# Gate, up and down of an adaLN block: where the last pair's operands, Wd's slices, Silu's products and down's first loads stand

## The chip, the cores and the metric

The kernel runs on one core of one Trainium2 chip, in one launch. The metric is the device time of that launch in microseconds, as the median of runs; all arithmetic is fp32.

## The reference

The kernel computes one transformer block with adaptive layer norm, for x of 2 × 1024 × 1024. Cut to what matters:

```python
mod = (silu(c) @ wmod).reshape(2, 6, 1, -1)
sa, ca, ga, sb, cb, gb = (mod[:, i] for i in range(6))
h = layernorm(x) * (1 + ca) + sa
x = x + ga * attention(h)               # 32 heads, causal, ALiBi slopes, clipped qkv, LN on q and k
h = layernorm(x) * (1 + cb) + sb
gate = einsum('bsh,ih->bsi', h, Wg) * ag        # Wg, Wu: 2752 x 1024
up = einsum('bsh,ih->bsi', h, Wu) * au
x = x + gb * (einsum('bsi,hi->bsh', silu(gate) * up, Wd) * ad)   # Wd: 1024 x 2752
```

(`ga` and `gb` are kept at least 0.25 away from zero.) The change touches the second half: gate, up and down.

## The kernel before

The large products are done by Strassen and Winograd's scheme with seven products in place of eight, in two levels: an outer one whose seven products are called stages (`STAGES`), and an inner one whose seven products run in the order of `CHAIN`. The reduction over 1024 becomes, for gate and up, stage by stage, products of a weight tile (an inner operand, made by `gate_inner` on GpSimd from the outer sums of `gate_sums`) with a 512 KB tile of h's operand.

**h's operands.** The tokens of h lie transposed in SBUF, in two batch halves (b = 0, 1) and pairs j = 0 to 3. For the outer operands T1 to T4 and B22 of a pair, `second_batch` (L1299) makes four half sums, and for each operand `inner_b` (L1156) makes four inner differences into a tile `inner` (two buffers) and stores all to DRAM (`bop_B..`, `bop_T..`). Pairs 0 to 2 share this between VectorE and GpSimd; the last one, `second(3, nc.vector)`, is called after the first weights' loads and does everything on VectorE. It runs in the pool `rest`, which also serves the rest rows (the 192 rows of the inner dimension of 2752 that the slabs do not cover), and which is closed before gate and up get their pools.

**Gate and up.** There are five slabs s of 512 of the inner dimension. Each has seven stages, and each stage seven inner products. One inner product is, for gate and for up, two matmuls of 128x128 by 128x512; both use one `bt` tile (`moving`, L1635, six buffers), loaded by SyncE except the first six, which ScalarE's queue loads. Banks are `gx, gy, ux, uy`, in two sets of four that alternate by stage. `merge` (L1560) reads a bank after its product: P1, U2 and P5 become parts (copied on ScalarE or added on VectorE, L1566 and L1568), the others become results X, C, Z and T (L1572, L1574, L1576). A bank's next product waits for the read.

**After a stage.** `after(n, go)` puts a closure into a queue that `run_due` empties n products later in program order. `final` (L1678) applies Silu on ScalarE (L1683) and the product on VectorE (L1684) to a finished result and stores it for down (`act_dram`, L1688). GpSimd makes T and Z from X (L1730, L1737). At the end of a slab eight act sums S1 to S4 (L1751) are made on VectorE and stored (L1752).

**Wd's slices.** Down needs outer sums of Wd. In twenty slices, one for each stage from the first, `down_load` (L1170) loads 512 KB into the single tile `wdr` with two DMAs, and `down_weights` (L1179), five products later, makes T1 to T4 into a second tile `wdo` on GpSimd (L1184 to L1187) and stores them with four DMAs (L1189), all on SyncE.

**Down.** Seven stages again; `stage_weights` (L1804) loads four operands of Wd and makes T1 to T4 of them, `products` (L1819) loads the activations `aq` (L1823), makes inner sums `dsi` on VectorE and issues seven groups of ten matmuls (L1843) of 128x256, for four i a stage.

What an engine does in which order is decided by a scheduler, which follows the data and may move an instruction past others of its engine. Only a helper fixes an order: `behind(ins, first)` makes `ins` stand behind `first` without a wait between engines. SyncE, like the other engines, works its instructions off in order: a DMA that must wait holds up all those behind it in that queue.

Of the kernel before, what the change touches and what calls it, by code (L numbers as in the profile page):

```python
# [18 lines left out]
P = 128  # L19
# [461 lines left out]
def kernel(  # L481
# [674 lines left out]
    def inner_b(o, block, j, pool, eng):  # L1156

        v = block.rearrange("p (q c) h t -> p q c h t", q=2)
        b11, b12, b21, b22 = v[:, 0, :, 0], v[:, 0, :, 1], v[:, 1, :, 0], v[:, 1, :, 1]
        t_ = pool.tile([P, 4, 2, P], FP, tag="inner", name=f"inner_{o}_{j}", bufs=2)  # L1160
        eng.tensor_sub(t_[:, 0], b12, b11)
        eng.tensor_sub(t_[:, 1], b22, t_[:, 0])
        eng.tensor_sub(t_[:, 2], b22, b12)
        eng.tensor_sub(t_[:, 3], b21, t_[:, 1])
        to = bop_dram[o]
        for r, src_ in ((0, b11), (1, b21), (2, b22)):
            nc.sync.dma_start(to[:, r, j], src_)
        nc.sync.dma_start(to[:, 3:7, j], t_)

    def down_load(i, pool):  # L1170

        s, c_ = i // 4, i % 4
        w = pool.tile([P, 4, 2, P], FP, tag="wdr", name=f"wdr_{i}")
        rows_ = wd_t[ds(s * 4 * P, 4 * P), :].rearrange("(j p) e -> p j e", p=P)
        for n in range(2):
            nc.sync.dma_start(w[:, :, n], rows_[:, :, ds(n * HALF + c_ * P, P)])
        return w

    def down_weights(i, w, pool):  # L1179

        s, c_ = i // 4, i % 4
        B11, B12, B21, B22 = (w[:, 2 * kh : 2 * kh + 2, n] for kh, n in ((0, 0), (0, 1), (1, 0), (1, 1)))
        ot = pool.tile([P, 4, 2, P], FP, tag="wdo", name=f"wdo_{i}")
        nc.gpsimd.tensor_sub(ot[:, 0], B12, B11)  # L1184
        nc.gpsimd.tensor_sub(ot[:, 1], B22, ot[:, 0])
        nc.gpsimd.tensor_sub(ot[:, 2], B22, B12)
        nc.gpsimd.tensor_sub(ot[:, 3], B21, ot[:, 1])  # L1187
        for r, o in enumerate(("T1", "T2", "T3", "T4")):
            nc.sync.dma_start(wd_dram[o][:, s, :, ts(c_, P)], ot[:, r])  # L1189
# [111 lines left out]
    def second_batch(j, pool, h0, h1, half):  # L1301

        oo = pool.tile([P, 2, KC // 2, 2, P], FP, tag="oo", name=f"oo_{j}")
        t1, t4, lo1, hi1 = h0[:, 0 : KC // 2], h0[:, KC // 2 :], h1[:, 0 : KC // 2], h1[:, KC // 2 :]
        t2, t3 = oo[:, 0], oo[:, 1]
        nc.vector.tensor_sub(t1, lo1, t1)
        nc.vector.tensor_sub(t2, hi1, t1)
        half.tensor_sub(t3, hi1, lo1)
        half.tensor_sub(t4, t4, t2)
        for o, v, eng in (  # L1310
            ("T2", t2, nc.vector), ("T1", t1, nc.vector), ("T3", t3, half),
            ("B22", hi1, nc.vector), ("T4", t4, half),
        ):
            inner_b(o, v, j, pool, eng)
# [73 lines left out]
    with ExitStack() as st:  # L1388
# [26 lines left out]
        def extra(todo, n):  # L1415
            if n in (1, 2, 5, 6):
                out_weights((1, 2, 5, 6).index(n), wosp)
            if n in (5, 7, 8, 9):
                tokens(1, (5, 7, 8, 9).index(n), todo, nxp, nxp, qpools[-1])
            if 4 <= n < 9:  # L1420
                late(todo, 7)
            if n == 3:
                loaded.extend(mod_load(wmr, nc.sync, *pieces[i]) for i in range(AHEAD))
                for b in range(B):
                    for q in range(2):
                        nc.sync.dma_start(adrow[64 + 32 * q + b, :], ad[ts(q, 512)])
            if n == 9:
                assert not left
                for g, ps in sums.items():
                    todo.add(  # L1430
                        lambda bank, g=g, ps=ps: mod_vectors(
                            g, ps, mrw, bank.rearrange("p (r c) -> p r c", r=4), adrow
                        )
                    )
# [57 lines left out]
    opools, _, bt, todo, _ = out_args  # L1492
    rest_st = ctx.enter_context(ExitStack())
    rest_pool = right["rest"] = rest_st.enter_context(tc.tile_pool(name="rest", bufs=1, side="right"))
    rps = rest_st.enter_context(tc.tile_pool(name="rest_ps", bufs=4, space=PSUM))

    def fetch(b, j, eng=nc.sync):
        kept[b, j] = rest_pool.tile(
# [7 lines left out]
    def second(j, eng=nc.gpsimd):  # L1506
        second_batch(j, rest_pool, kept[0, j], kept[1, j], eng)
# [51 lines left out]

    def merge(q, bank, to, frm, part_t, pool, nm):  # L1560

        if q in ("P1", "U2", "P5"):
# [4 lines left out]
            else:  # L1567
                nc.vector.tensor_add(part_t[q], frm(m, n), bank)  # L1568
            return
        m, n = QUAD[q]  # L1570
        if q != "U6":
            nc.vector.tensor_add(to(m, n), part_t[MATE[q]], bank)  # L1572
        elif frm is None:
            nc.scalar.copy(to(m, n), bank)  # L1574
        else:
            nc.vector.tensor_add(to(m, n), frm(m, n), bank)  # L1576

    with ExitStack() as ff:
# [9 lines left out]
        with ExitStack() as gu:  # L1588
# [4 lines left out]
            wbp, wap, bsp, wip, wlp = open_("wbb"), open_("wba"), open_("bst", 6), open_("wis", 2), open_("wlast")  # L1593
# [41 lines left out]
            def moving(s, n_, i, eng=nc.sync):  # L1635
# [9 lines left out]
            second(3, nc.vector)  # L1645
            rest_st.close()
            ffp.append(ff.enter_context(tc.tile_pool(name="ff_a", bufs=4, space=PSUM)))
            ptp, rxp, rcp, rzp, asp, dwp = (
                open_("fpart"), open_("resx"), open_("resc"), open_("resz"), open_("asum"), open_("wdsum")
            )  # L1650
# [4 lines left out]
            def after(n, go):  # L1655

                queue.append((count[0] + n, go))
                queue.sort(key=lambda e: e[0])

            def run_due(all_=False):  # L1660
                while queue and (all_ or queue[0][0] <= count[0]):
                    queue.pop(0)[1]()

            for s in range(NSB):
# [5 lines left out]
                def result(mat, x_):  # L1670
                    if (mat, x_) not in res:
                        res[mat, x_] = {"X": rxp, "C": rcp}.get(x_, rzp).tile(
# [5 lines left out]
                def final(x_, m, q, res=res, s=s):  # L1678

                    g, u = res["g", x_], res["u", x_]  # L1680
                    for l in range(2):
                        ib = 4 * s + 2 * m + l
                        nc.scalar.activation(g[:, l], g[:, l], AF.Silu, scale=vt[:, R_AG + ib : R_AG + ib + 1])  # L1683
                        nc.vector.scalar_tensor_tensor(  # L1684
                            u[:, l], u[:, l], vt[:, R_AU + ib : R_AU + ib + 1], g[:, l], ALU.mult, ALU.mult
                        )
                    if q != "A21":
                        nc.sync.dma_start(act_dram[q][:, s], u)  # L1688

                for n_, (oa, ob, frm, to) in enumerate(STAGES):  # L1690
                    if (s, n_) != (0, 0):
# [12 lines left out]
                    if i is not None:  # L1704
                        wd_ = down_load(i, dwp)
                        after(5, lambda i=i, wd_=wd_: down_weights(i, wd_, dwp))
# [18 lines left out]
                    if oa == "A12":  # L1725
                        after(1, lambda: final("C", 0, "A11"))
# [6 lines left out]
                    elif oa == "S3":  # L1733
# [4 lines left out]
                        after(4, lambda: final("Z", 1, "A22"))  # L1738
                    elif oa == "S4":
                        after(1, lambda: final("T", 0, "A21"))  # L1740
                    elif oa == "A22":
                        after(1, lambda final=final: final("X", 1, "A12"))

                a11, a12, a21, a22 = (res["u", x_] for x_ in ("C", "X", "T", "Z"))
                for l in range(2):
# [4 lines left out]
                    def go(q, op, dst, x_, y_, s=s, l=l):  # L1750
                        op(dst, x_, y_)  # L1751
                        nc.sync.dma_start(act_dram[q][:, s, l], dst)  # L1752

                    for e, (q, op, dst, x_, y_) in enumerate((
# [5 lines left out]
                        after(2 + (4 * l + e) // 2, lambda go=go, r=(q, op, dst, x_, y_): go(*r))  # L1760
# [3 lines left out]
        with tc.tile_pool(name="aq", bufs=3) as aqp, tc.tile_pool(name="wdq", bufs=1) as wdp, tc.tile_pool(  # L1764
# [39 lines left out]
            def stage_weights(ob):  # L1804
                wt = {
                    q: (wtp if q[0] == "T" else wdp).tile(
# [4 lines left out]
                for q, l, c_ in (("B11", 0, 0), ("B12", 0, 1), ("B21", 1, 0), ("B22", 1, 1)):  # L1811
                    nc.sync.dma_start(wt[q], down_operand(ob, l, c_))
# [6 lines left out]
            def products(n_, i, wt):  # L1819
# [3 lines left out]
                nc.sync.dma_start(  # L1823
# [57 lines left out]
            for n_ in range(len(STAGES)):  # L1881
                wt = stage_weights(STAGES[n_][1])
# [62 lines left out]
```

## Time and profile before

| | |
|---|---|
| time, three runs | 2995.03, 2987.3, 2984.26 us, median 2987.3 |
| profiled execution | 2987.97 us, span 2986.3, mean granted clock 0.965 |
| TensorE busy | 2739.7 us (92%) |
| VectorE, ScalarE, GpSimd busy | 1476.0 (49%), 687.2 (23%), 1277.0 us (43%) |
| DMA | 579.12 MB, mean 194 GB/s |
| gate and up on TensorE | 1554.71 to about 2474.4 us |
| first matmul of down | 2490.28 us |

All positions are in microseconds from the start of the profiled span. In a timeline a row gives the start, the duration, the engine, the line of the kernel, the operation, its output and input tiles, and in brackets how long the engine had been idle and what ended that. In the list of costly groups the last columns are the busy time of the group, the mean of one in nanoseconds, and the idle time ahead of it with the releaser. PE is TensorE, DVE VectorE, ACT ScalarE, POOL GpSimd, SP SyncE.

### The profile page before, as it was taken

To read this page: it belongs to the slowest core of one execution; us is meant where nothing else is said; L and a number is where in the kernel's file an instruction comes from. 1 tells how busy PE (TensorE), PEld (TensorE's weight loads), DVE (VectorE), ACT (ScalarE), POOL (GpSimd) and SP (SyncE) were. 2 spreads that over 40 slices of the span, in tenths; PEclk is the share of its full clock that TensorE was granted. 3 is DMA by queue.
4 is the path that set the end of the run, shared out by engine and by line. 5 is a ranking of instruction groups with operands and counts; after the bars stand their busy time and mean duration, and the time that the engine had idled before them with its cause. 6 is when DMAs were issued, how large, how long until landed. Compare 5 with 4: busy or idle time off the path is not lost. (4 is left out here: it accounts for less than half of the span.)

```text
span 2986.3 us, 29722 instructions
## 1 busy us (share of the span) xinstructions
PE 2739.7 (92%) x10271; PEld 1339.0 (45%) x10271; DVE 1476.0 (49%) x2295; ACT 687.2 (23%) x1523; POOL 1277.0 (43%) x1140
## 2 busy tenths in 40 slices
PE   7999899999998888888997869999999997999998
PEld 2444333333332222224563324444444446888776
DVE  5666424566453456564564333453535354444553
ACT  1322144444434455553111001010101100000000
POOL 3211033334354555564555556564635540222343
PEclk9999999999999899999998989999999998999999
DMA  9777762534535445334777778675766658555542
GB/s 347 278 269 290 273 210 98 186 136 162 182 109 187 140 152 156 115 113 131 226 247 227 240 246 276 187 276 169 270 183 229 197 176 258 159 143 141 152 141 79
DMA packets 376931, 579.12 MB, mean 194 GB/s; under 512 B 20950, under 2 KB 278072, under 8 KB 365636
## 3 DMA queue, kind: packets, MB, share of 16 engines
q1 hardware_dynamic: 366904, 559.78, 57.5%
q10 hardware_dynamic: 9868, 17.35, 1.8%
q8 instruction: 84, 1.38, 0.2%
q14 instruction: 75, 0.61, 0.1%
HBM read 411.89 MB, written 165.17 MB: 193 GB/s over the span
## 5 line engine op out<-in xcount | busy, mean ns | idle before, releaser
L1053 ACT ACTIVATE p<-sc,kw 128x128 f32<-128x128 f32 (+3 forms) x1024 | 422.1, 514 | 335.1 <-PE sc L745 320.2
L1085 POOL TENSOR_TENSOR p<-p,p 128x1024 f32<-128x1024 f32 (+3 forms) x128 | 265.3, 2072 | 255.8 <-PE av L745 227.1
L745 PE MATMUL bank<-wT,a 128*128 128x512 f32 x768 | 361.4, 613 | 13.6 <-DVE wT L814 6.8
L1085 DVE TENSOR_TENSOR p<-p,p 128x1024 f32<-128x1024 f32 (+3 forms) x192 | 248.8, 1309 | 118.1 <-POOL p L1057 69.7
L745 PE MATMUL bank<-wB,a 128*128 128x512 f32 x576 | 265.0, 604 | 2.7 <-DVE raw L947 2.2
L745 PE MATMUL sc<-cq,ck 32*128 32x512 f32 (+3 forms) x1536 | 198.3, 557 | 68.9 <-ACT p L1053 68.5
L1057 POOL TENSOR_SCALAR_AFFINE_SELECT p<-p 128x256 f32<-128x256 f32 x256 | 136.6, 544 | 227.3 <-ACT p L1053 224.4
L745 PEld LDWEIGHTS bank<-wT,a 128*128 128x128 f32 x768 | 141.8, 194 | 200.3 <-issue 177.2
L745 PE MATMUL av<-p,cv 128*32 128x512 f32 (+3 forms) x1536 | 170.5, 513 | 3.9 <-POOL p L1057 3.9
L745 PEld LDWEIGHTS bank<-wB,a 128*128 128x128 f32 x576 | 104.8, 191 | 148.1 <-issue 129.6
L1712 PE MATMUL gx<-bt,sig 128*128 128x512 f32 x280 | 135.4, 607 | 31.6 <-DVE g_P L1568 18.3
L1712 PE MATMUL gy<-bt,sig 128*128 128x512 f32 x280 | 135.3, 606 | 25.6 <-DVE gX L1572 20.6
L745 PEld LDWEIGHTS sc<-cq,ck 32*128 32x128 f32 x1536 | 66.2, 190 | 201.7 <-ACT p L1053 118.5
L1712 PE MATMUL ux<-bt,siu 128*128 128x512 f32 x280 | 134.6, 604 | 2.2 <-DVE u_U L1568 1.1
L1712 PE MATMUL uy<-bt,siu 128*128 128x512 f32 x280 | 132.3, 595 | 0.0
L949 DVE TENSOR_TENSOR raw<-P,bank 128x512 f32<-128x512 f32 x48 | 32.9, 686 | 159.8 <-PE bank L745 157.5
L1712 PEld LDWEIGHTS gx<-bt,sig 128*128 128x128 f32 x280 | 53.3, 192 | 101.4 <-issue 99.7
L1712 PEld LDWEIGHTS gy<-bt,sig 128*128 128x128 f32 x280 | 53.7, 194 | 95.4 <-issue 72.1
L745 PEld LDWEIGHTS av<-p,cv 128*32 128x32 f32 x1536 | 33.3, 110 | 120.9 <-issue 86.8
L1712 PEld LDWEIGHTS ux<-bt,siu 128*128 128x128 f32 x280 | 54.3, 195 | 73.7 <-issue 70.3
L1712 PEld LDWEIGHTS uy<-bt,siu 128*128 128x128 f32 x280 | 53.8, 192 | 68.3 <-issue 67.3
L1712 PE MATMUL gx<-bt,wgS 128*128 128x512 f32 x160 | 75.4, 593 | 2.1 <-DMA bt<-bop_B 1.1
(418 smaller groups left out, 4516.1 us busy)
## 6 DMA issues: line engine op xcount, KB each, us to landing
bt<-bop_T SPq DMA_DIRECT2D x140, 512.0 KB
bt<-bop_B SPq DMA_DIRECT2D x99, 512.0 KB
a<-hop SPq DMA_DIRECT2D x20, 1792.0 KB
wm<-in_L_wmod_dram SPq DMA_DIRECT2D x48, 512.0 KB
wB<-in_L_attn_Wqkv_dram SPq DMA_DIRECT2D x21, 1024.0 KB
aq_S<-act_S SPq DMA_DIRECT2D x16, 1280.0 KB
qk<-qs SPq DMA_DIRECT2D x16, 1024.0 KB
act_S<-asS SPq DMA_DIRECT2D x30, 512.0 KB
```

What stands on the lines that cost most here:

```text
L745: return in_order(nc.tensor.matmul(*args, **kw_))
L949: nc.vector.tensor_add(dst, part_t[MATE[q]], bank)
L1053: nc.scalar.activation(p[:, g, lo:hi], sp[:, g, lo:hi], AF.Exp, bias=kw[:, d, h_ : h_ + 1])
L1057: nc.gpsimd.affine_select(out=p[:, :, 0:P], in_=p[:, :, 0:P], pattern=[[0, 2], [1, P]], compare_op=ALU.is_ge, fill=0.0, base=0, channel_mu ...
L1085: adders[b](half, jb).tensor_add(dst, dst, ps[half][:, :, 0:n])
L1712: nc.tensor.matmul(ps.rearrange("p (j t) -> p j t", j=NJ), ins[mat][qa][:, c2, :], bt[:, :, c2, :], start=(q in ("P1", "P2", "P5") and c2 ...
```

## The change

Six things move.

1. The last pair's operands (`second_batch` for j = 3) are no longer made in one go ahead of gate and up. The function now returns two lists of closures. Those on VectorE (T1, T2, B22) come due from the first product on, one a product, and their first instruction is put `behind` the last read of a bank (`last_read`). Those on GpSimd (T3, T4) come due from the eighth product on. The pair's tiles live in a pool `pair` of their own, closed before stage 2.
2. Wd's slices are made in place: `wdr` has five slots, the four differences overwrite what they no longer need, and the stores read from `wdr`. The load is four DMAs in place of two. The pool of the slices is opened first, ahead of `bt`'s.
3. `final` splits into Silu, due after n products, and the product, due one product later; the product and the act sums are put `behind` the last read.
4. Down's first weights (`stage_weights` of stage 0) and its first two activations go through ScalarE's queue; the order of the loads is B11, B21, B12, B22; B12 moves to another pool, and `wdq` opens before `aq`.
5. The first loads for the modulation come at turn 2 in place of 3 of the attention's helper.
6. `resz` and `asum` are opened at stage 2 of the first slab.

In the order of the changed kernel, as built, VectorE does the second product's reads first, then one half sum, T1's and T2's inner differences and one of B22, then the fifth product's reads. GpSimd does slice 0 before the last rest rows' sums, and the differences of slices 1 and 2 behind the eight weight sums. On SyncE the order there is: stores of slice 1, loads of slice 2, the seventh `bt`, stores of slice 2, the first `bt` of stage 1; slice 3's loads stand at the first `bt` of stage 2, slice 16's at the fourth `bt` of slab 1.

```diff
-        w = pool.tile([P, 4, 2, P], FP, tag="wdr", name=f"wdr_{i}")
+        w = pool.tile([P, 5, 2, P], FP, tag="wdr", name=f"wdr_{i}")
-        for n in range(2):
-            nc.sync.dma_start(w[:, :, n], rows_[:, :, ds(n * HALF + c_ * P, P)])
+        for kh in range(2):
+            for n in range(2):
+                nc.sync.dma_start(w[:, 2 * kh + n], rows_[:, 2 * kh : 2 * kh + 2, ds(n * HALF + c_ * P, P)])
...
-    def down_weights(i, w, pool):
+    def down_weights(i, w):
...
-        ot = pool.tile([P, 4, 2, P], FP, tag="wdo", name=f"wdo_{i}")
-        nc.gpsimd.tensor_sub(ot[:, 0], B12, B11)
-        nc.gpsimd.tensor_sub(ot[:, 1], B22, ot[:, 0])
-        nc.gpsimd.tensor_sub(ot[:, 2], B22, B12)
-        nc.gpsimd.tensor_sub(ot[:, 3], B21, ot[:, 1])
-        for r, o in enumerate(("T1", "T2", "T3", "T4")):
-            nc.sync.dma_start(wd_dram[o][:, s, :, ts(c_, P)], ot[:, r])
+        nc.gpsimd.tensor_sub(w[:, 0], w[:, 1], w[:, 0])
+        nc.gpsimd.tensor_sub(w[:, 4], w[:, 3], w[:, 0])
+        nc.gpsimd.tensor_sub(w[:, 1], w[:, 3], w[:, 1])
+        nc.gpsimd.tensor_sub(w[:, 2], w[:, 2], w[:, 4])
+        for o, r in (("T1", 0), ("T2", 4), ("T3", 1), ("T4", 2)):
+            nc.sync.dma_start(wd_dram[o][:, s, :, ts(c_, P)], w[:, r])
...
-            second(3, nc.vector)
+            on_dve, on_pool = second_batch(3, pair_pool, kept[0, 3], kept[1, 3])
+            for e, go in enumerate(on_dve):
+                after(1 + e, go)
+            for e, go in enumerate(on_pool):
+                after(8 + e, lambda go=go: (go(), None)[1])
...
             def run_due(all_=False):
                 while queue and (all_ or queue[0][0] <= count[0]):
-                    queue.pop(0)[1]()
+                    read = last_read[0]
+                    ins_ = queue.pop(0)[1]()
+                    if ins_ is not None and read is not None:
+                        behind(ins_, read)
...
+                    for l in range(2):
+                        after(n, lambda l=l: silu(l))
+                    for l in range(2):
+                        after(n + 1, lambda l=l: product(l))
...
-                        after(4, lambda: final("Z", 1, "A22"))
+                        final("Z", 1, "A22", 5)
...
-                        after(2 + (4 * l + e) // 2, lambda go=go, r=(q, op, dst, x_, y_): go(*r))
+                        after(3 + (4 * l + e) // 2, lambda go=go, r=(q, op, dst, x_, y_): go(*r))
...
-                for q, l, c_ in (("B11", 0, 0), ("B12", 0, 1), ("B21", 1, 0), ("B22", 1, 1)):
-                    nc.sync.dma_start(wt[q], down_operand(ob, l, c_))
+                for q, l, c_ in (("B11", 0, 0), ("B21", 1, 0), ("B12", 0, 1), ("B22", 1, 1)):
+                    eng.dma_start(wt[q], down_operand(ob, l, c_))
...
-                nc.sync.dma_start(
+                (nc.sync if n_ or i > 1 else nc.scalar).dma_start(
...
-            if n == 3:
+            if n == 2:
                 loaded.extend(mod_load(wmr, nc.sync, *pieces[i]) for i in range(AHEAD))
```

## The prediction

> **What bounds the kernel now.** I read the page's table of busy time first, then its costliest groups, then TensorE's waits between 1555 and 2475 us (gate and up), then the timelines of VectorE, SyncE and TensorE around each long wait.
>
> ```profile
> PE 2739.7 (92%) x10271; PEld 1339.0 (45%) x10271; DVE 1476.0 (49%) x2295; ACT 687.2 (23%) x1523; POOL 1277.0 (43%) x1140
> ...
> L1712 PE MATMUL gx<-bt,sig 128*128 128x512 f32 x280 | 135.4, 607 | 31.6 <-DVE g_P L1568 18.3
> L1712 PE MATMUL gy<-bt,sig 128*128 128x512 f32 x280 | 135.3, 606 | 25.6 <-DVE gX L1572 20.6
> ```
>
> TensorE is busy 92% of the span, and the change leaves its matmuls alone. So only TensorE's idle time, and the slow matmuls behind it, can be won. Gate and up have some 62 us of it. The waits say where.
>
> ```profile
> PE gy L1712 <- DVE gX L1572: 20.6, 1, 20.6
> PE gx L1712 <- DVE g_P L1568: 18.3, 1, 18.3
> PE gx L1712 <- issue: 7.4, 3, 2.5
> PE gx L1712 <- DMA bt<-bop_T: 5.3, 2, 3.5
> PE gy L1712 <- DMA bt<-bop_B: 4.1, 1, 4.1
> PE gx L1712 <- DMA bt<-bop_B: 3.5, 2, 2.4
> ```
>
> Two single waits on VectorE make 38.9 us; waits on `bt` make 13. The first, on VectorE's timeline:
>
> ```profile
> 1562.91 2.57 DVE L1162 TENSOR_TENSOR inner_T<-hl,inner_T 128x256 f32<-128x256 f32 x1
> 1565.40 2.56 DVE L1163 TENSOR_TENSOR inner_T<-hl 128x256 f32<-128x256 f32 x1
> ...
> 1580.62 0.41 DVE L1163 TENSOR_TENSOR inner_B<-h2t 128x256 f32<-128x256 f32 x1
> ...
> 1585.00 0.69 DVE L1572 TENSOR_TENSOR gX<-g_P,gy 128x512 f32<-128x512 f32 x1
> ```
>
> TensorE has waited since 1565.17 for that read. Ahead of it stand the last pair's twenty inner differences: 0.41 us alone, 2.56 us beside GpSimd's eight weight sums (2.52 us each, until 1580.09).
>
> The second wait ends the ladder of Wd's slices. SyncE, in order, shows one round of it (lines of other tiles left out):
>
> ```profile
> 1664.77 1.00 SPq L1176 DMA_DIRECT2D wdr<-in_L_ffn_Wd_dram  x2
> ...
> 1671.22 2.25 SPq L1189 DMA_DIRECT2D wdop_T<-wdo  x3
> ...
> 1674.50 0.36 SPq L1189 DMA_DIRECT2D wdop_T<-wdo  x1
> 1674.96 1.14 SPq L1176 DMA_DIRECT2D wdr<-in_L_ffn_Wd_dram  x2
> ```
>
> A round is load, four GpSimd differences, four stores, next load: 10.2 us here. Between the loads at 1598.76 and 1750.93 lie 14 rounds, 10.9 us each. The `bt` loads stand in the same queue, about 2.7 a round, and a product eats one in 3.43 us (9.3 us a round): hence the `bt` waits. GpSimd's `uZ` sums stand behind the same rounds, VectorE's product behind `uZ`, and the read that TensorE needs behind that product: 18.3 us, until 1769.97.
>
> Last, the seam to the down product:
>
> ```profile
> 2484.04 3.49 SPq L1812 DMA_DIRECT2D wd_B_B<-in_L_ffn_Wd_dram  x4
> ...
> 2490.28 4.61 PE L1843 MATMUL dx<-wd_B_B,aq_A 128*128 128x256 f32 x10 [15.84 <-issue]
> ```
>
> The weights' loads are issued behind act-sum stores that wait for VectorE, and land six us later.
>
> The times come from the profiled execution: 2987.97 us with a span of 2986.3, 0.7 us above the median 2987.3. The sum is made against 2987.97; 0.5%, about what a measurement of this kernel tells from no change, is 15 us.
>
> **Step 1: start of gate and up.** In the order of the changed kernel VectorE reads the second product first, and then does two half sums and nine inner differences before the fifth product's read. So the wait at the fourth product goes. What is late next is the seventh product's `bt`, which now stands on SyncE behind slice 1's stores and slice 2's loads. GpSimd does the last pair's T3 half sum (2.4) and then the eight sums: done about 1582.5. Slice 1's four differences (0.69 each) end 1585.2, their last store is issued 1585.3 and lands 3.0 us later (the inner store issued 1580.39 landed in 3.00), at 1588.3. Slice 2 takes four loads of 0.45: 1590.1. Then the seventh `bt`: the loads issued at 1700.42, 1720.09 and 1741.67 let TensorE go 3.4, 3.0 and 2.9 us later, so I take 3.0. The seventh product starts about 1593.1 (before 1598.68). VectorE's nine differences, even at 2.56, are done by 1588 and are covered by that; without the cover they would cost the same wait to 1588. Slice 2 lands 6.4 us after its first issue, 1594.7; differences and stores end about 1598; stage 1's first `bt` is issued at 1598.4. Stage 1 starts at 1601.4 (before 1602.12). **−1 us**: the stall moves more than it goes. The other end is −14, if GpSimd's list starts sooner; +3, if slice 0's added megabyte (1520 to 1540 shows a DMA share of 1.00 at 341 GB/s, so 3 us) holds up the last rest rows.
>
> **Step 2: the ladder with the slice made in place.** The next load overwrites the tile that the stores read, so a round now holds a store's landing, and SyncE waits in it with `bt` loads queued behind. A round by rows: first issue to first difference was 5.2 to 5.9 us, mostly; two more issues make 6.4 (5.8 to 6.75). Four differences take 2.8 alone, and 4.5 on the mean of the nine rounds from 1670 with what GpSimd does between: 3.6. Last store's issue 0.4, its landing 3.0, release 0.1. Sum **13.5 us**. The landing is unseen for a 128 KB store: from below 3.0 less 1.15 us for 384 KB at 341 GB/s, 1.85; from above some 4.5, since the same stretch has DMA shares of 0.63 to 0.90 and stores in the saturated one took 10. So a round lies between 11.0 and 16.2; I stay by the one landing seen.
>
> The Trainium skill (DMA: Bandwidth & Descriptors, section "Anatomy of one DMA") has about 2.0 us fixed for each DMA, most of it the receipt of the write, plus bytes at 436 GB/s; it speaks against this edit too, but more mildly: 2.3 us a landing, an estimate, so a round of 12.8, and a total 9 us lower. The row of 3.00 stays.
>
> Slice 3's load stands at the eighth product past stage 1's first, so it can go at 1601.4 + 3.4 = 1604.8. Thirteen rounds later (slice 16) stands the `bt` of slab 1's fourth product: 1604.8 + 175.5 = 1780.3, plus issue 0.4, landing 3.0, and 3 us for slow matmuls after stalls (the wait of 3.45 at 1723 made 2.92 and 2.66 of 1.88): 1786.7. Before, that product started at 1796.68. **−10 us**, step 1 included, the 18.3 us wait gone (products and sums are now pinned behind reads, and GpSimd's Z sums no longer block them), the `bt` waits longer. Without any stall TensorE would be there at 1601.4 + 45 × 3.43 = 1755.8 (−41); 16.2 us a round gives 1821.8 (+25).
>
> **Step 3: slices 17 to 19.** Three more longer rounds that stand among stage starts: 3 × (13.5 − 10.9) = 8, half of it behind `bt`s loaded ahead: **+4 us** (0 to 8).
>
> **Step 4: pinned products and sums.** The three "issue" waits, 7.4 us at the slab ends, go. But two products (1.28) and a sum (1.22) of the old slab now fall between two reads of the next slab's first stage: 3.8 us in a gap that is 1.03 us in the trace, so the read is 2.8 late. The other pair of banks gives part of that back; I take half, 1.4, four times, 5.6. **−2 us** (−7 to +4).
>
> **Step 5: the seam.** Three of the first weights' loads and the first operands go to ScalarE's queue, which reaches them after Z's Silu, about 2455; only B12 waits for the last Silu. Gate and up end about 2474.5. TensorE has six groups of ten down matmuls at once (2.16 each at full clock, 13 us), then waits for VectorE's last product, eight sums (1.22 each), T1 and T2 (1.5 each), until about 2494.5, where before its second kind of group started 2498.54 on a slow clock. I take **−11 us**: of the 15.84 us wait some 5 stay. Bounds −15 and −3, if ScalarE's queue is held by a buffer.
>
> **Step 6: modulation loads one turn earlier.** Seven loads (three of 512 KB, issued 133.71, 0.7 us each) move ahead of others on SyncE. TensorE waited 7.3 us for `wm` in two places and up to 1.6 us around 135 for what stands behind: **0** (−3 to +2).
>
> Sum: −10 + 4 − 2 − 11 + 0 = −19; 2987.97 − 19 = 2969.
>
> **The rivals.** *Slower: the ladder's round.* One mechanism: the store's landing, in a busy DMA stretch, added to every round while SyncE's `bt`s queue behind. At 16.2 us a round the fourth product of slab 1 comes 25 us late, slices 17 to 19 cost 8, and steps 4 and 5 return 13: +20, 3008. It decides from about 15 us a round on (zero) and 16 (slower by 0.5%). For it: the `bt` waits already there at 10.9. Against it: the one landing seen took 3.00. Chance 0.22.
>
> *Nothing to speak of: the stalls only move.* Start stall to the seventh product, end-of-slab stall into 14.3 us rounds (0 against before), seam alone pays: 2976 to 2990. For it: step 1's walk. Chance 0.28.
>
> *Much faster: rounds of 12 us.* Then 13 × 1.5 = 20 us more come: 2949, with the start's −14 down to 2940. For it: light GpSimd lists in half of the rounds (2.9 us for four differences). Chance 0.20.
>
> *The seam's loads do not start early*, because their region is still read by the last slab: then −3 instead of −11: 2977. Chance 0.06, inside the second.
>
> **How the numbers follow.** My forecast (rounds near 13.5, seam open) has 0.30 and 2960 to 2976; with the fast rival 0.50 for faster by over 15 us, and 0.28 for within 15; 0.22 for slower. The range runs from the fast rival's lower third, 2942, to the slower rival's price, 3008: about 0.06 lies below and 0.11 above.
>
> **What would show it.** Right: TensorE's wait on `gX` at the fourth product gone, and one on `bt` at the seventh, ending about 1593; Wd loads 12.5 to 14.5 us apart from 1605 on, waits on `bt` in every stage of slab 0, no wait near 18 us on `g_P`; the first down matmul under 3 us behind the last of gate and up. Wrong: rounds under 12 or over 15.5 us; a wait on VectorE of over 5 us at a slab's first stage; Wd's first loads on ScalarE's queue later than 2475.

## The result, and the profile after

| | before | after |
|---|---|---|
| median of four runs each | 2989.47 us (2984.26 to 2995.03) | 3008.64 us (3005.75 to 3011.73) |
| ratio, 95% interval | | 1.0064, 1.0042 to 1.0086 |
| span of the profiled execution | 2986.3 us | 3007.6 us |

The change makes the kernel 0.6% slower; the forecast was 0.6% faster. In the kernel after, matmuls stand at L1744 (before: L1712), reads at L1578 and L1582 (L1568, L1572), Silu's product at L1707 (L1684), act sums and their stores at L1783 and L1784 (L1751, L1752), slices at L1179 to L1190, down's matmuls at L1876 (L1843). The page's table of busy time and its costly groups, the lines that answer to those of before:

```profile
PE 2743.3 (91%) x10271; PEld 1341.0 (45%) x10271; DVE 1506.9 (50%) x2285; ACT 686.6 (23%) x1523; POOL 1289.1 (43%) x1150
...
L1744 PE MATMUL gy<-bt,sig 128*128 128x512 f32 x280 | 139.4, 622 | 27.4 <-DVE gX L1582 13.2
```

TensorE does the same work, with 3.6 us more busy time; VectorE is busy 31 us longer with ten instructions fewer, so its instructions have become slower. TensorE's waits from 1500 to 2500 us (engine, tile and line, and what it waited for; total, times, longest):

```profile
PE gx L1744 <- DVE gX L1582: 27.9, 1, 27.9
PE gy L1744 <- DMA bt<-bop_B: 26.4, 6, 11.5
PE gy L1744 <- DVE gX L1582: 13.2, 3, 4.5
PE gx L1744 <- DMA bt<-bop_T: 4.9, 5, 1.8
```

Against before, the two single waits of 20.6 and 18.3 us are gone, and so are the "issue" waits at the slab ends. In their place stand one of 27.9 at the start, 26.4 on `bt`, and 13.2 in three waits on a read.

Where TensorE loses and gains is read from the start of the same product in both timelines. A row gives how much later than before a kernel is there, in one profiled execution each (stages are counted from 0; the later kernels are told of below):

| point on TensorE | before, us | after | early_pair | unpinned | prod_free | sums_free | spread_after | before_spread | groups_aq_sync |
|---|---|---|---|---|---|---|---|---|---|
| gate and up start | 1554.71 | +0.5 | −0.9 | +0.7 | −0.3 | −3.1 | −0.6 | −1.1 | −4.1 |
| slab 0, stage 1 | 1602.12 | +8.4 | +0.4 | +9.7 | +8.4 | +3.0 | −8.2 | −0.8 | −23.2 |
| slab 1, start | 1789.81 | −24.2 | −24.5 | −6.1 | −7.4 | −31.7 | −51.7 | −40.8 | −56.7 |
| slab 1, stage 2 | 1837.88 | +5.3 | +3.3 | −6.1 | −2.2 | −3.2 | −37.0 | −40.8 | −55.9 |
| last row of gate and up | 2472.56 | +22.9 | +23.1 | −5.4 | −1.1 | +39.1 | −15.9 | −41.1 | −54.1 |
| first down matmul | 2490.28 | +6.9 | +7.1 | −16.1 | −15.5 | +23.0 | −31.8 | −41.1 | −68.9 |
| 71st down matmul | 2508.11 | +22.9 | +22.5 | −0.5 | −0.5 | +37.6 | −15.0 | −39.9 | −63.2 |

So after: start +8.4, rest of slab 0 −32.6, first two stages of slab 1 +29.5, slabs 1 to 4 behind that +17.6, seam 0, what follows −1.6: +21.3, the difference of the spans. One column has some scatter: kernels whose code up to gate and up is that of after start it between −4.1 and +5.2 us, so what counts is the change from row to row, and a few microseconds say little.

**The start.** VectorE's timeline:

```profile
1582.42 0.94 DVE L1165 TENSOR_TENSOR inner_T<-oo,inner_T 128x256 f32<-128x256 f32 x1
...
1602.82 0.43 DVE L1164 TENSOR_TENSOR inner_B<-h2t 128x256 f32<-128x256 f32 x1 [19.46 <-DMA bop_T<-inner_T]
1603.16 0.68 DVE L1582 TENSOR_TENSOR gX<-g_P,gx 128x512 f32<-128x512 f32 x1
```

SyncE's and TensorE's:

```profile
1589.17 0.47 SPq L1650 DMA_DIRECT2D bt<-bop_B  x1
...
1596.45 1.01 SPq L1169 DMA_DIRECT2D bop_T<-inner_T  x2
```

```profile
1603.90 3.78 PE L1744 MATMUL gx<-bt,wgA 128*128 128x512 f32 x4 [27.87 <-DVE gX L1582]
```

Eight inner differences are done at 1583.4. The ninth, B22's first, needs a third `inner` tile, and there are two: it waits until T1's operand has landed in DRAM, and T1's store stands on SyncE (issued 1596.45) behind slice 1's stores, slice 2's loads, the seventh `bt` and slice 2's stores. The fifth product's read is behind that difference, and TensorE's seventh product, whose `bt` was issued at 1589.17, starts at 1603.90.

**Slab 1's first stages.** SyncE's queue (lines of other tiles left out; a row of several instructions runs from the first one's start to the last one's end, waits included):

```profile
1777.39 0.47 SPq L1650 DMA_DIRECT2D bt<-bop_B  x1
1786.44 0.36 SPq L1190 DMA_DIRECT2D wdop_T<-wdr  x1
...
1788.45 3.27 SPq L1650 DMA_DIRECT2D bt<-bop_B  x3
...
1792.97 1.34 SPq L1784 DMA_DIRECT2D act_S<-asS  x2
...
1796.58 13.60 SPq L1784 DMA_DIRECT2D act_S<-asS  x3
...
1815.21 3.36 SPq L1650 DMA_DIRECT2D bt<-bop_B  x6
```

The timelines of GpSimd, VectorE and TensorE:

```profile
1778.59 1.77 POOL L1640 TENSOR_TENSOR sig<-wgA 128x256 f32<-128x256 f32 x1
...
1783.65 0.72 POOL L1638 TENSOR_TENSOR siu<-wuA 128x256 f32<-128x256 f32 x1
...
1785.69 0.72 POOL L1186 TENSOR_TENSOR wdr<-wdr 128x256 f32<-128x256 f32 x1
```

```profile
1803.56 2.98 DVE L1783 TENSOR_TENSOR asS<-uT,uZ 128x1024 f32<-128x1024 f32 x1 [17.73 <-DMA act_S<-asS]
```

```profile
1796.65 3.75 PE L1744 MATMUL gy<-bt,sig 128*128 128x512 f32 x4 [11.55 <-DMA bt<-bop_B]
1819.86 3.75 PE L1744 MATMUL gy<-bt,wgA 128*128 128x512 f32 x4 [10.39 <-DMA bt<-bop_B]
```

It is one chain. From 1777.9 to 1786.4 SyncE stands at slice 16's second store, because GpSimd's difference for it ends only at 1786.4: ahead of it stand seven inner weight sums, four of 1.58 to 1.77 us beside VectorE's products and act sums, three of 0.72, the same size, once VectorE has stopped. The slowing makes some 3.9 us of these 8.5; the rest is the place behind seven sums. The `bt` behind that store costs TensorE 11.55 us. The first half's act sums were done by 1783.1, but their stores go out only from 1792.97; the second half's first sum overwrites the tile that the first of them reads and waits for its landing until 1803.56. Its stores then hold SyncE until 1815.1, and the `bt` loads behind them cost another 10.39 us.

**Slabs 2 to 4.** VectorE's timeline at slab 2's start:

```profile
1970.44 0.69 DVE L1582 TENSOR_TENSOR uX<-u_P,uy 128x512 f32<-128x512 f32 x1 [5.18 <-issue]
1971.05 4.95 DVE L1707 SCALAR_TENSOR_TENSOR uX<-uX,vt,gX 128x1024 f32<-128x1024 f32 x2
1975.92 3.35 DVE L1783 TENSOR_TENSOR asS<-uT,uZ 128x1024 f32<-128x1024 f32 x1
1979.20 0.67 DVE L1582 TENSOR_TENSOR gX<-g_P,gy 128x512 f32<-128x512 f32 x1
```

GpSimd's timeline at that moment:

```profile
1974.88 3.32 POOL L1630 TENSOR_TENSOR wgS<-wgA,wgS 128x1024 f32<-128x1024 f32 x1
```

TensorE's:

```profile
1979.93 3.78 PE L1744 MATMUL gy<-bt,sig 128*128 128x512 f32 x4 [4.43 <-DVE gX L1582]
```

Two products and a sum stand between two reads, as forecast, but they take 4.95 + 3.35 = 8.3 us, not 3.8: a product is 2.48 instead of 1.28, a sum 3.35 instead of 1.22, and GpSimd's weight sum 3.32 instead of 2.35. TensorE waits 4.43, 4.29 and 4.49 us for the read at 1979.20 and its two likes.

The Trainium skill (SBUF — State Buffer, section "Who interferes with whom") says that a VectorE instruction with two inputs in SBUF contends with a GpSimd instruction that reads SBUF, and one with a single such input does not. The trace agrees on who is hit: reads of a bank, with one input in SBUF, keep 0.67 to 0.69 us beside the same GpSimd sums. On how, the page has the second instruction blocked until the first ends. Here the records of both become longer, which two streams that wait for each other in turn would show as well; the prediction's differences of 0.41 us that take 2.56 beside sums of 2.52 look like blocking. No run here parts blocking from sharing inside one instruction.

### The profile page after: what moved, and what is told of

Its sections match the earlier page's. It is cut to its first block, busy times and chain, and to the rows that moved or that the text cites. A ratio compares the mean times of both kernels' runs of the same rounds, so it can differ in the third digit from the quotient of the medians.

```text
span 3007.6 us, 29795 instructions
## 1 busy us (share of the span) xinstructions
PE 2743.3 (91%) x10271; PEld 1341.0 (45%) x10271; DVE 1506.9 (50%) x2285; ACT 686.6 (23%) x1523; POOL 1289.1 (43%) x1150
## 4 chain that ended last, share of the span: by engine, by line
PE 39%; DMA 7%; POOL 6%; issue 5%; DVE 3%; ACT 1%; SPq 1%; POOLq 0%; ACTq 0%; DVEq 0%
PE gx L1744 7%; PE ux L1744 6%; PE dx L1876 6%; PE dy L1876 5%; PE gy L1744 5%; PE uy L1744 4%; PE bank L745 2%; PE sc L745 1%; DMA wdr<-in_L_ffn_Wd_dram 1%; ACT p L1053 1%; DMA wdop_T<-wdr 1%; PE rest L745 1%; DMA bt<-bop_B 1%; PE av L745 1%; POOL p L1085 1%
## 5 line engine op out<-in xcount | busy, mean ns | idle before, releaser
L1744 PE MATMUL gy<-bt,sig 128*128 128x512 f32 x280 | 139.4, 622 | 27.4 <-DVE gX L1582 13.2
L1744 PE MATMUL gx<-bt,sig 128*128 128x512 f32 x280 | 134.9, 605 | 4.4 <-DMA bt<-bop_T 2.3
L1744 PE MATMUL uy<-bt,siu 128*128 128x512 f32 x280 | 132.2, 594 | 0.6 <-DMA bt<-bop_B 0.6
L1744 PE MATMUL ux<-bt,siu 128*128 128x512 f32 x280 | 131.6, 592 | 0.0
L1744 PEld LDWEIGHTS gy<-bt,sig 128*128 128x128 f32 x280 | 54.6, 198 | 98.7 <-issue 80.4
L1744 PEld LDWEIGHTS gx<-bt,sig 128*128 128x128 f32 x280 | 54.2, 196 | 76.9 <-issue 74.6
L1744 PE MATMUL gx<-bt,wgA 128*128 128x512 f32 x120 | 58.4, 610 | 28.5 <-DVE gX L1582 27.9
L1744 PEld LDWEIGHTS uy<-bt,siu 128*128 128x128 f32 x280 | 53.5, 191 | 68.7 <-issue 68.0
L1744 PEld LDWEIGHTS ux<-bt,siu 128*128 128x128 f32 x280 | 53.2, 190 | 67.0 <-issue 66.3
```

What stands on the lines that cost most here:

```text
L1744: nc.tensor.matmul(ps.rearrange("p (j t) -> p j t", j=NJ), ins[mat][qa][:, c2, :], bt[:, :, c2, :], start=(q in ("P1", "P2", "P5") and c2 ...
```

## The experiments

All kernels below are the kernel after with the edit shown, but for seam_only and before_spread, which start from the kernel before.

**unpinned.** Silu and product in one closure as before, nothing of it behind a read.

```diff
-                    for l in range(2):
-                        after(n, lambda l=l: silu(l))
-                    for l in range(2):
-                        after(n + 1, lambda l=l: product(l))
+                    after(n, all_)              # silu(l), product(l) for l = 0, 1
-                        final("Z", 1, "A22", 5)
+                        final("Z", 1, "A22", 4)
-                        r = op(dst, x_, y_)
+                        op(dst, x_, y_)         # and no "return r"
-                        after(3 + (4 * l + e) // 2, ...)
+                        after(2 + (4 * l + e) // 2, ...)
```

> After with products and act sums as before: due as early as before, in one closure, and not put behind a read; all else as after. Theory A (the late, pinned products and sums cost at every slab start, because SyncE's bt loads queue behind the sums' stores, and fill VectorE at the seam): slabs 1 to 4 lose under 8 us in place of 47, the seam gains, 2970 to 2990, though the wait of some 18 us at the end of slab 0 may come back. Theory B (the slices made in place are what costs): 3003 to 3013 as after. Theory C (only the start costs): 3003 to 3013.

Measured: 2981.79 us, ten runs, 0.9995 (0.9985 to 1.0005). The whole loss is gone, and with it the gain in slab 0: the wait that the change removes is back.

```profile
PE gx L1746 <- DVE gX L1582: 28.7, 1, 28.7
PE gx L1746 <- DVE g_P L1578: 17.1, 1, 17.1
```

The other edits, in place slices and all, cost nothing in sum.

**early_pair.** The last pair all on VectorE ahead of gate and up, as before.

```diff
-            on_dve, on_pool = second_batch(3, pair_pool, kept[0, 3], kept[1, 3])
...
+            second(3, nc.vector)
             rest_st.close()
```

> After with the last pair's operands made at once, all on VectorE ahead of gate and up, as before; all else as after. Theory C (the pair in groups costs at the start, as its third inner tile waits for the first one's store and the read of the fifth product stands behind it): stage 1 starts at 1602 in place of 1610.5, 2998 to 3003. Theories A and B: the start matters little, since the ladder's head decides: 3005 to 3012.

**early_two.** The same, and slices from `wdr` into a tile `wdo` with two loads, as before.

```diff
-        w = pool.tile([P, 5, 2, P], FP, tag="wdr", name=f"wdr_{i}")
+        w = pool.tile([P, 4, 2, P], FP, tag="wdr", name=f"wdr_{i}")
...
+        ot = pool.tile([P, 4, 2, P], FP, tag="wdo", name=f"wdo_{i}")
```

> As early_pair, and the slices with two tiles and two loads as before (the pair's pool closes early, which makes the room). Against early_pair: theory B (a round of the slice ladder is longer in place) 10 to 20 us faster; theory A: within 5 us, since the rounds of after are 10.9 us on the mean as those of before.

Measured: 3008.68 (1.0082, 1.0063 to 1.0101) and 3013.94 (1.0105, 1.0086 to 1.0124). Without the groups the start is won back (+0.4 at stage 1 against +8.4), yet slab 1 starts at the same moment, −24.5: the ladder swallows it. And a separate tile does not help; by the medians it is 5 us the slower, with intervals that overlap. So the slice in place, the step that I feared most, costs nothing here.

**seam_only.** The kernel before with the new seam alone (queue, order and pools of down's first loads).

> Before with the seam alone changed: down's first weights and first two activations through ScalarE's queue, B12 in another pool, wdq opened first. My step 5: 8 to 14 us faster than before, 2973 to 2981. If VectorE's work at the seam is what is late next anyway (after shows 11.65 us of wait on dsi there): within 4 us of before.

Measured: 2997.97 (1.0052, 1.0033 to 1.0071). The four runs are 2985.68, 3001.82, 2999.71 and 2996.22, and the profiled one is the first. In it the last row of gate and up is 5.6 us early and the 71st down matmul 1.9, so the seam itself loses 3.7 us, and TensorE's wait ahead of down is still 14.62 us. Where the other three lost 10 to 16 us more the trace does not show; that stays open.

**sums_free** and **prod_free.** The two halves of the pinning: only the act sums freed, with the products still behind reads; only the products (with Silu) freed, with the sums still behind reads.

> After with the act sums as before (due one product earlier, not behind a read, and Z's product due one product earlier too); products stay behind reads. Theory A1 (the eight sums behind reads are the cost: their stores hold SyncE, and the second S1 waits for the first one's store): most of the 27 us goes, 2980 to 2988. Theory A2 (the products behind reads are the cost, as all sums depend on the late uX and uZ products): 3000 to 3012.

> After with Silu and product in one closure as before, not behind a read; the sums stay behind reads. Theory A1: 3000 to 3012. Theory A2: 2980 to 2988. If both share: about 2995 in each of the two.

Measured: sums_free 3029.91 (1.0149, 1.0108 to 1.0190; its edit leaves Z's product at its later due time, unlike the text ahead of the run); prod_free 2989.03, ten runs, 1.0000 (0.9983 to 1.0017), with this wait:

```profile
PE gx L1746 <- DVE g_P L1578: 19.2, 1, 19.2
```

It is the products. With them behind reads, freeing the sums makes it worse (+39.1 at the end of gate and up): waits of `gx` and `gy` on `bt<-bop_B` make 42.2 us, in after 28.5. What holds these loads longer was not followed up. With them free, and the sums still behind reads, slab 1's first two stages lose 5.2 us where after loses 29.5, and the slabs behind 1.1 where after loses 17.6; the 19.2 us wait on `g_P` at slab 0's end is back, which makes 16.8 us at slab 1's start.

**not_behind.** The products keep their later due time and closures, but not their place behind a read.

```diff
                         if l and q != "A21":
                             nc.sync.dma_start(act_dram[q][:, s], u)
-                        return r
```

> After with the products due as in after, in closures of their own, but not put behind a read; the sums stay behind reads. If the order behind the read is the cost: 2982 to 2992, as prod_free. If the later due time is: 3002 to 3012, as after.

Measured: 2987.98, ten runs, 0.9988 (0.9977 to 1.0000); the end of gate and up is at +4.2 instead of +22.9, and the wait of 19.1 us on `g_P` at slab 0's end is back. One deleted line turns 0.6% slower into no change that this measurement can tell. It is the place behind the read, not the due time.

**unpinned_early.** unpinned and early_pair together.

> unpinned with the last pair made at once on VectorE as well, so of the change only the slices in place, the seam, the pools' order and the modulation loads are left. Theory C (the pair in groups costs 8 to 9 us at the start): stage 1 starts at 1602 in place of 1611.8 and the total is 6 to 9 us under unpinned, about 2974. If the ladder of slices decides slab 0, as early_pair suggests: stage 1 early, but slab 1 starts as in unpinned, about 2982.

Measured: 2985.55, ten runs, 0.9987 (0.9969 to 1.0006): the start's edit is worth nothing as long as the ladder follows.

**spread.** unpinned_early, and each slice's loads ordered behind the last `bt` load of the stage before, so that no slice runs ahead of its stage.

```diff
+                d_ = nc.sync.dma_start(w[:, 2 * kh + n], ...)
+                if last is not None:
+                    behind(d_, last)
...
-                eng.dma_start(bt, bop_dram[...])
+                last_bt[0] = eng.dma_start(bt, bop_dram[...])
...
-                        wd_ = down_load(i, dwp)
+                        wd_ = down_load(i, dwp, last_bt[0] if i else None)
```

> unpinned_early with each slice's loads put behind the last bt load of the stage before (no wait, order on SyncE alone), so one slice a stage for twenty stages in place of sixteen in slab 0. Theory D (the packed ladder of slices sets slab 0, through bt loads queued behind its stores and GpSimd's Z sums behind its differences, whatever is done in it): the bt waits of slab 0 and the wait of 17 us at its end go, slab 1 starts at 1772 or earlier, total 2950 to 2965. Rival (the slices only move their cost into later stages): 2975 to 2985.

Measured: 2953.52 (0.9890, 0.9851 to 0.9929). SyncE now loads one slice a stage, as at 1676.34 and 1700.38, 24 us apart. Of the long waits in slab 0 only that of the start stays (19.1 us); the `bt` waits and the one at the slab's end are gone.

**before_spread.** The kernel before with this edit alone.

> Before with the slices' loads one a stage, nothing else of the change. Theory D (the packed ladder costs slab 0 some 35 us): slab 0's bt waits and the 18 us wait go, 2948 to 2960, as spread: then the rest of the change is worth little. If the slices in place and the other edits carry part of spread's gain: 2962 to 2975.

Measured: 2947.85 (0.9854, 0.9832 to 0.9876). All of it comes in slab 0: −0.8 at stage 1, −40.8 at slab 1's start, and flat from there. That the scheduler let sixteen slices run in the time of slab 0 is the largest cost that these runs found in the kernel before; the next run has the same edit on the kernel after.

**spread_after.** The kernel after with this edit alone, its products and sums still pinned.

> After with one slice a stage, products and sums still behind reads. Theory A3 (products behind reads cost by their own lateness: reads wait behind the sums, SyncE's stores behind the sums, bt behind the stores): the losses at the starts of slabs 2 to 4, some 6 to 9 us each, stay, and slab 1 loses about as much; 2970 to 2985. Rival (they cost only together with the ladder's tail at slab 1): 2950 to 2960, as spread.

Measured: 2972.19 (0.9940, 0.9916 to 0.9964). Its longest waits:

```profile
PE gy L1748 <- DVE gX L1584: 17.8, 5, 4.4
PE gx L1748 <- DVE gX L1584: 13.1, 1, 13.1
PE gy L1748 <- DMA bt<-bop_B: 11.6, 4, 4.7
PE dx L1880 <- DVE dsi_A L1867: 10.2, 1, 10.2
```

Without a ladder the pinning has little to gain and much to lose. At slab 1's start this kernel is at −51.7, spread at −42.0, and 6.3 us of that difference stand at stage 1 already, where the place of the last pair is what differs. From there to the end of gate and up, −15.9, it gives away 35.8 us, where spread gives away 1.9 (to −40.1).

**act_stores.** After, with the act stores on ScalarE's queue.

> After with the stores of the products and of the act sums on ScalarE's queue in place of SyncE's. If SyncE's order is the path (bt behind stores that wait for late sums): the waits on bt of 11.6 and 10.4 us at slab 1 go or fall under 4, 2985 to 2998, unless ScalarE, now held by the same waits, is late with its copies; then waits on ScalarE show in their place and the time stays at 3000 to 3015. If VectorE's order alone is the path: 3003 to 3012, bt waits gone, waits on gX grown.

Measured: 3013.52 (1.0065, 1.0041 to 1.0089). The waits of `gy` on `bt<-bop_B` fall from 26.4 us to 5.9, so the stores did hold up SyncE. But slab 1's stage 2 comes at +21.0, later than in after: the wait moves to ScalarE, whose copies of P1 now stand behind those stores. The store just ahead of this copy, and what the profile names as the end of the wait, a slice's store:

```profile
1790.12 0.35 ACTq L1711 DMA_DIRECT2D act_A<-uZ  x1
1790.57 0.59 ACT L1576 COPY g_P<-gx 128x512 f32<-128x512 f32 x1 [15.54 <-DMA wdop_T<-wdr]
```

**asum_two.** After, with a second buffer for the first act sum S1 alone.

```diff
-  q: asp.tile([P, 2, 512], FP, tag=q, name=f"as{q}_{s}_{l}") for q in ("S1", "S2", "S4")
+  q: asp.tile([P, 2, 512], FP, tag=q, name=f"as{q}_{s}_{l}", bufs=2 if q == "S1" else 1) for q in (...)
```

> The kernel after with two buffers for the act sum S1 (the tile that the first store of a half reads). In after, slab 1's second half of sums starts only at 1803.56, when the first half's store, issued at 1792.97, has landed; the stores of the second half then hold SyncE until 1815.21, and TensorE waits 10.39 us for the bt behind them. Theory: this one buffer carries the second of the two bt waits of slab 1. Then the sum goes ahead at about 1787, the hold of 13.60 us falls under 5, the 10.39 us wait goes, slab 1's stage 2 comes at about -5 instead of +5.3 against before, and the time falls by 8 to 11 us, to about 2999. Rival: the stores wait for the other sums (S2 and S4 have one buffer each) or for the products' late order anyway: then the hold stays near 13 us and the time within 3 us of 3008.6. The first wait, 11.55 us behind slice 16's second store, stays with both, and so do the three waits of 4.3 to 4.5 us at slabs 2 to 4.

Measured: 3007.03, five runs, 1.0058 (1.0039 to 1.0078): the rival's outcome in time. The S1 sum of the second half runs ahead, at 1781.94, and the S2 sum takes over its wait, for its own tile's store, until 1801.92. The stores hold SyncE 10.29 us instead of 13.60, TensorE waits 8.77 instead of 10.39. Second buffers for all three tiles were not tried, so how much of slab 1's 29.5 us these buffers make in all stays open.

**spread_groups**, **groups_seam_back**, **groups_aq_sync.** Towards the best: spread with the last pair in groups again, due at products 1, 1, 3, 8, 11 on VectorE and 9 to 12 on GpSimd; that with before's seam; that with the new seam, but the first two `aq` loads on SyncE.

```diff
-                (nc.sync if n_ or i > 1 else nc.scalar).dma_start(
+                nc.sync.dma_start(
```

> spread with the last pair in groups again, T2 due at the eighth and B22 at the eleventh product so that neither stands ahead of the fifth product's read; products and sums free. If the third inner tile ahead of a read was what cost at the start: the wait of 19.1 us on gX in spread goes to under 6, total 2935 to 2945. If the start is bound by other work (bt of stage 1, weight sums): 2948 to 2958.

> spread_groups with the seam as before (pools, queue, order). From the ledgers the stretch from the last gate and up matmul to the seventieth of down takes 41.5 us in spread_groups and 36.7 in before_spread, so 3 to 6 us faster: 2931 to 2935. If the two seams are alike: 2936 to 2939.

> spread_groups with the first two activations' loads on SyncE again, weights still on ScalarE's queue. If the activations' long way on ScalarE's queue (issue to use over 20 us) is what fails in the seam: the waits of 10.8 us on aq go, 2925 to 2932. If T1 and T2 (B12's load) come late in any case: 2934 to 2938.

Measured: 2937.40 (0.9820, 0.9788 to 0.9853), 2932.27 (0.9812, 0.9790 to 0.9834) and 2921.74 (0.9771, 0.9748 to 0.9795). Once no ladder follows, the groups at the start, worth nothing before, are worth 16 us by the medians (with these due times); the two intervals just touch, and the two profiled executions are 8 us apart. The seam's edit parts into two: the weights through ScalarE's queue, with the new order and pools, gain 10.5 us over before's seam, the activations there lose 15.7, by the medians. The waits of groups_aq_sync:

```profile
PE gx L1750 <- issue: 9.8, 4, 2.5
PE gy L1750 <- DMA bt<-bop_B: 4.6, 3, 3.4
PE dx L1881 <- DVE dsi_A L1868: 3.5, 1, 3.5
```

No single wait longer than 3.5 us is left there, from the start of gate and up into down. This version beats both kernels, by 2.3% the one before.

## Why the prediction was wrong

Only its upper end, 3008, which it had for the slower rival, is near the measured time, and that by luck: the rival's mechanism did not happen. A round of the ladder took 11.8 us, against 16.2 for the rival, 13.5 for the forecast and 10.9 before. The steps that failed:

**Step 4, pinned products and sums (−2 forecast): the term that decided.** The place was right, products and a sum in a gap of 1.03 us ahead of a read. Mis-sized was their price. I took 1.28 and 1.22 us, durations from where they stood before, out of GpSimd's way; where the pin puts them, GpSimd sums weights, and the same three instructions take 8.3 us, so that TensorE waits 4.3 to 4.5 at slabs 2 to 4 where I had 1.4. And I priced only VectorE: that GpSimd gets slower too, and that a slice's store, the act stores and `bt` loads queue behind it on SyncE, is missing from the step. After against prod_free has the products' place and due time as the difference (not_behind shows that the place decides): 16.8 us won at slab 1's start, then 24.3 lost in its first two stages and 16.5 in the slabs behind, net 24.0 at the end of gate and up. Without a ladder, products and sums together cost 33.9 from slab 1's start on (spread_after against spread).

**Step 1, start (−1 forecast, +8.4 measured).** "VectorE's nine differences ... are covered" failed at the ninth. (One of the two half sums that I put with them ran ahead of gate and up, at 1546.29.) I had looked at the durations, and not at the two buffers of `inner`, whose release is a store queued on SyncE. The row that gave the forecast its landing of 3.00 us had that wait in it, 1.06 us long, in the kernel before:

```profile
1583.42 0.43 DVE L1161 TENSOR_TENSOR inner_T<-hl 128x256 f32<-128x256 f32 x1 [1.06 <-DMA bop_T<-inner_T]
```

The stall moved to the seventh product, as forecast, but ends at 1603.9 instead of 1593.1, on VectorE and not on `bt`. It cost nothing in the end (early_pair's time is after's).

**Step 2, the ladder (−10 at slab 1's fourth product; −18.7 measured).** The sign was right, the size too low: between the loads of slice 3, at 1618.06, and slice 16, at 1771.33, are 13 rounds of 11.8 us, not 13.5 (below 12, a sign that I had listed against the forecast). Two terms of the round were too long. From a slice's first load to its first difference I had 6.4 us; the mean of the 13 rounds is 4.9 (6.3 in the kernel before). By the code the first difference needs two of the four new loads only. For the last store's issue, its landing and the release I had 3.5 us. From that issue to the next load:

```profile
1734.21 0.36 SPq L1190 DMA_DIRECT2D wdop_T<-wdr  x1
1737.06 1.91 SPq L1179 DMA_DIRECT2D wdr<-in_L_ffn_Wd_dram  x4
```

2.85 us here; the 13 rounds have 1.9 to 6.3, 2.75 on the mean. The four differences took 3.9 us, about the 3.6 that I had, and 0.3 passes before the last store. The Trainium skill's estimate in the prediction, 2.3 us a landing, makes 2.8 with issue and release and is nearer; its section "Anatomy of one DMA" gives the figures for DMAs on GpSimd's path, and these stores stand on SyncE. The 18.3 us wait did go, because the products no longer stand behind GpSimd's Z sums: prod_free and not_behind bring it back. That was the gain of the pins, and it is smaller than their cost. Of step 3's slices 17 to 19 (+4) no run has the cost by itself.

**Step 5, the seam (−11 forecast, 0 measured).** The first half came true: TensorE goes into down without a wait, the first down matmul 1.7 us after the start of gate and up's last row (before 17.7), 16 us won. The second half failed. TensorE:

```profile
2504.33 4.11 PE L1876 MATMUL dx<-wd_B_B,aq_A 128*128 128x256 f32 x10 [2.64 <-DMA aq_A<-act_A]
...
2526.56 4.61 PE L1876 MATMUL dx<-wd_B_T,dsi_A 128*128 128x256 f32 x10 [11.65 <-DVE dsi_A L1863]
```

I had TensorE wait for VectorE until 2494.5; with the 22.9 us by which all is late that is 2517.4, and it waits to 2526.6: the pinned Z products run only from 2494.62, sums and reads follow in a heap, and in it VectorE waits 4.55 us for the last weight, whose load ScalarE's queue issued at 2497.38:

```profile
2513.28 1.49 DVE L1846 TENSOR_TENSOR wd_B_T<-wd_B_B,wd_B_B 128x1280 f32<-128x1280 f32 x1 [4.55 <-DMA wd_B_B<-in_L_ffn_Wd_dram]
```

With the products free, in unpinned, 15.6 us are still given back, now 10.8 on `aq` and 5.4 on T's sums. The `aq` loads on ScalarE's queue are the other half: from the last row of gate and up to the 71st down matmul, groups_aq_sync, with them on SyncE, wins 9.1 us against before (−54.1 to −63.2), where spread_groups loses 5.5 (−49.8 to −44.3), and the waits on `aq` fall from 10.8 to 1.8.

**Right:** step 6 (gate and up start at +0.5, within the scatter). The chance of 0.22 for slower rested on the ladder alone: the pins, which made the kernel slower, had a range of −7 to +4, drawn from rows without their neighbours.

## What to carry to other kernels

An instruction that is fixed in an in-order engine's list must be priced where it lands: with what the neighbouring engines run at that time, and followed to its own stores and to all that queues behind these. Before a stall is shaved at one place, look for the thing that sets the next place; here sixteen prefetches packed into the first slab swallowed the gain made ahead of them, and ordering each behind the `bt` loads of the stage before was worth more, 1.5%, than all six edits. Buffers of a small helper tile, two for `inner`, are a wait too, and no duration shows it.

## What was not expected of the hardware

The issue of a DMA can itself hold a queue. On ScalarE's, in the kernel after, at the seam:

```profile
2473.84 1.61 ACTq L1845 DMA_DIRECT2D wd_B_B<-in_L_ffn_Wd_dram  x3
2475.61 14.03 ACTq L1856 DMA_DIRECT2D aq_A<-act_A  x2
...
2497.38 1.27 ACTq L1845 DMA_DIRECT2D wd_B_B<-in_L_ffn_Wd_dram  x1
```

The two `aq` issues took 1.65 and 12.35 us, with no wait that the profile names. From 2475 to 2490 the DMA engines were busy throughout (mean share 1.00, 304 GB/s); that this is what holds the issue is not shown. The slab's last two Silus (2493.03 and 2498.70) and the last weight stand behind them in that queue. The second issue ended at 2489.65 and the first Silu waited for VectorE until 2493.0, so the hold cost that one nothing; of the others the rows do not say it. Three such issues on SyncE took 13.00 us in groups_aq_sync, where these Silus and weights are not behind them. And VectorE and GpSimd slow each other down by more than I had thought: the same sum takes 1.22 or 3.35 us, while reads of a bank keep their duration.
